# A four-layer transformer on one core: layer 1's attention placed beside the last expert outputs of layer 0

## The chip, the cores and the metric

The kernel runs on one core of a Trainium2 chip. The metric is the device time of one execution in microseconds (us); less is better. The engines are named as in the profile: PE (TensorE, matmul and transposition), DVE (VectorE), ACT (ScalarE), POOL (GpSimd, which here issues the indirect DMAs), SP (SyncE, which here only issues DMAs).

## What is computed

Input and output are 16 sequences of 256 tokens with 128 features, fp32. Four layers follow each other, each of the form x + mixer(norm(x)) + feedforward(norm(x)), with a norm that has no weights. The norm divides by a square root, and so does the one inside layer 0's mixer:

```python
def _layernorm(x, axis=-1, eps=1e-05):
    m = jnp.mean(x, axis=axis, keepdims=True)
    v = jnp.var(x, axis=axis, keepdims=True)
    return (x - m) / jnp.sqrt(v + eps)
```

- Layer 0: the mixer is a linear state-space recurrence over each sequence, feature by feature, followed by `W_out` and a bias `b_out`; it amounts to a causal convolution. The feed-forward part is a mixture of eight SwiGLU experts, two per token, with weights from a softmax over gate logits, and a ninth expert that is shared by all tokens.
- Layer 1: causal attention with 16 heads of 8, and a SwiGLU part with int8 weights that arrive as int32 and are scaled by 1/127.
- Layer 2: attention over a window of three tokens, and a feed-forward part with ternary weights.
- Layer 3: causal attention again, and a small coupling network, applied three times.

## The kernel before

The 4,096 tokens lie in SBUF for the whole time as eight blocks `X[i]` of 128 partitions x 4 x 128; a block holds two sequences. `HALVES` are blocks 0 to 3 and 4 to 7. A token group (one of the 4 columns of a block) has 128 tokens, so a half has 16 groups, called n. `xT[i]` is the transposed, normalised block, 128 features x 512 tokens, which feeds the projections and feed-forward matmuls.

The order of work:

1. `lag_weights` and `lag_sums` (L359 to L405) make the convolution's kernel: exponentials on ACT, products on DVE, matmuls `lag` on PE, eight copies `kt` (L395) on DVE, and a round trip through DRAM. `toeplitz` (L410) loads back a block of it in shifted form by SP's queue into a buffer with tag `toe`, of which there are five.
2. `prepare` (L192 to L239) makes for each half the statistics (`stats`, L113) and the inverse standard deviation (`inv_std`, L105: add, a square root on ACT, L109, a reciprocal on DVE), then a second norm factor `r1` and an offset `off` for the convolution's input Z, each in a chain of small DVE and ACT operations. ACT forms Z, PE transposes it (`zT`), and PE multiplies by the gate weights (`lg`). When all eight blocks have logits, `route` (L247) computes the slots of every token in a sorted buffer of 23 tiles of 256 slots per half, nearly all of it on DVE, with `tot` and `pos` on PE. Then ACT makes the normalised `xn` (L234), PE transposes it and ACT copies it to `xT`.
3. `scatter` (L341) writes the groups of `xn` into the sorted buffer `XS` by indirect DMA on POOL, one per group and choice.
4. A loop over eight blocks: `conv(q)` (L416), then `shared_expert(q)` (L438), while SP loads the next Toeplitz blocks.
5. The expert loop over 46 jobs (23 tiles x 2 halves). Step k issues a scatter of the second half (the first 17 steps), `fetch_weights(k + 4)` (L457, POOL, tag `we`, five buffers), from step 24 on `fetch_outputs(0, k - 24)` (L509: two indirect gathers from `YS` into buffers `yk`, on POOL), `fetch_slots` on SP, transpositions of the input, gate and up matmuls, in eight of the steps `mixed` (L524: the convolution's result times `W_out`, started by a matmul of the bias row with a row of ones), and `down_slots` (L492 to L505), which stores the outputs to `YS` on SP's queue. `combine` (L517) adds weighted outputs to X on DVE, two operations per group.
6. After the loop: 32 gathers and 16 combines for the second half.
7. The weight packs of layers 2 and 3 (L602 to L604, SP's queue), layer 1's integer weights `pk1i` (L829, POOL's queue) and their conversion (L833, three DVE operations); `norm_half` (L607) for both halves.
8. `attention` (L618) over 16 sequences s of layer 1 in a software pipeline: in step s it makes the maxima of sequence s (scores on PE, `M` reduced on DVE, L712, in three steps), the exponentials of s - 1 (scores again on PE, `E` on ACT, L754) and the context of s - 2. Then the SwiGLU part, and layers 2 and 3, which keep their form.

In the stages 4, 5 and 8 the order of PE, ACT, DVE is that of the program text (`manual_schedule`; in 4 and 5 SP too, in 5 POOL too); an engine takes its instructions strictly in that order. In the others a scheduler sets the order when the kernel is built. A DMA is issued by the engine whose queue it is on, in that engine's order.

Of the kernel before, what the change touches and what calls it, by code (L numbers as in the profile page):

```python
# [18 lines left out]
P = 128  # L19
B, S, D = 16, 256, 128  # L20
NBLK = 8
NT = 4
# [11 lines left out]
PK0 = dict(log_a=64, bpar=64, cpar=64, log_dt=64, dpar=32, lns=1, lnb=1, gate=8, gamma=128, beta=128, wout=128)  # L34
# [17 lines left out]
def program(ctx: ExitStack, tc: tile.TileContext, x, consts, consts0, rows, pk0, w0s, w0e, pk1, pk1i, pk2, pk3, out):  # L52
# [27 lines left out]
    def load(pool, src, spec, name, dt=F32, eng=None):  # L80
        cols, n = columns(spec)
        t = pool.tile([P, n], dt, tag=name, name=name)
        (eng or nc.gpsimd).dma_start(out=t, in_=src)
        return {k: t[:, s] for k, s in cols.items()}
# [9 lines left out]
    row = cp.tile([1, 3, D], F32, tag="row", name="row")  # L94
# [10 lines left out]
    def inv_std(pool, mv, n, name):  # L105

        r = pool.tile([P, n], F32, tag="rstd", name=name)
        nc.vector.tensor_scalar(r, mv[:, :, 1], EPS, None, ALU.add)
        nc.scalar.activation(r, r, AF.Sqrt)  # L109
        nc.vector.reciprocal(r, r)  # L110
        return r
# [42 lines left out]


    with banks(8, 0), tc.tile_pool(name="l0w", bufs=1) as wp, tc.tile_pool(name="l0", bufs=2) as sp:
# [10 lines left out]

        order = mybir.DependencyInfo(mybir.DependencyClass.NoSync, mybir.DependencyReason.DATA)
# [23 lines left out]
        def prepare():  # L192
# [6 lines left out]
            for hf, blocks in enumerate(HALVES):  # L199
# [4 lines left out]
                r1, off, off0 = (small(k, hf, HN) for k in ("r1", "off", "off0"))  # L204
# [3 lines left out]
                nc.scalar.activation(r1, r1, AF.Sqrt)  # L208
                nc.vector.reciprocal(r1, r1)
                nc.vector.tensor_tensor(r1, r1, r, ALU.mult)  # L210
                nc.vector.scalar_tensor_tensor(off, mv[:, :, 0], -1.0, r1, ALU.mult, ALU.mult)
                nc.vector.scalar_tensor_tensor(off0, mv[:, :, 0], -1.0, r, ALU.mult, ALU.mult)
                made.append((r, off0))
# [15 lines left out]
            routed = route(logits)  # L229
            for i in range(NBLK):  # L230
                r, off0 = made[i // 4]
                for t in range(NT):
                    k = i % 4 * NT + t
                    nc.scalar.activation(  # L234
                        xn[i][:, t, :], X[i][:, t, :], AF.Identity, bias=off0[:, k : k + 1], scale=r[:, k : k + 1]
                    )
                ps = transpose4(xn[i], f"xnT{i}")
                nc.scalar.copy(xT[i], ps)
            return xn, *routed  # L239
# [7 lines left out]
        def route(logits):  # L247
# [8 lines left out]
            m1, m2 = (wp.tile([P, N], F32, tag=k, name=k) for k in ("m1", "m2"))  # L256
# [58 lines left out]
            si = wp.tile([P, 2, N], I32, tag="slots", name="slots")  # L315
# [94 lines left out]
        def toeplitz(g):  # L410

            toes[g] = sp.tile([P, 4, 256], F32, tag="toe", name=f"toe{g}", bufs=5)
# [24 lines left out]

        def shared_expert(i):  # L438
# [18 lines left out]
        def fetch_weights(k):  # L457
            hf, j = jobs[k]
            w = live.setdefault(k, {})
            w["w"] = sp.tile([P, 6, 128], F32, tag="we", name=f"we{k}", bufs=5)  # L460
# [35 lines left out]
        def down_slots(k):  # L496
# [8 lines left out]
            nc.sync.dma_start(out=YS[hf][j * SLOTS : (j + 1) * SLOTS, :].rearrange("(t p) d -> p t d", p=P), in_=ys)  # L505
# [18 lines left out]
        def mixed(i):  # L524
            po = bank(f"po0_{i}")
            mm(po, ones, row[:, 0, :].unsqueeze(1).to_broadcast([1, NT, D]), True, False)
            for t in range(NT):
                mm(po[:, t * P : (t + 1) * P], yT[:, t % 2, 2 * i + t // 2, :], W0["wout"], False, t == NT - 1)
# [5 lines left out]
        xn, top, slots, rows_of, routed = prepare()  # L534
        for i in range(NBLK):
            affine(i)
# [11 lines left out]
        with tc.manual_schedule(engines=ordered):  # L548
            for g in range(4):
                toeplitz(g)  # L550
            for q in range(8):
                for g in range(4 * q + 4, min(4 * q + 8, 32)):
                    blocks_in = toeplitz(g)
                conv(q)
                add = nc.vector.tensor_tensor(X[q], X[q], xn[q], ALU.add)
                if q == 0:
                    tc.add_manual_dep(add.ins, routed.ins.name, order, reason="slots first")
                shared_expert(q)
            yT = wp.tile([P, 2, B, P], F32, tag="Z", name="yT")
# [5 lines left out]
        with tc.manual_schedule(engines=ordered | {mybir.EngineType.Pool}):  # L565
# [8 lines left out]
            up_slots(0)  # L574
            for k in range(NJ):
# [4 lines left out]
                out = k - TILES - 1  # L580
                if 0 <= out < HN:
# [580 lines left out]
```

## Time and profile before

| what | value |
|---|---|
| median of 3 runs | 1648.8 us (1647.44 to 1653.97) |
| the profiled execution | 1574.13 us, span 1572.4 us |
| mean granted TensorE clock in it | 0.935 |
| slots of all tokens ready (end of routing) | 76.9 us after the span's start |
| first expert matmul | 144.64 us |
| last expert matmul ends | 304.65 us |
| first reduction of a score maximum of layer 1 | 386.39 us |
| one sequence of layer 1's attention | 16.4 to 16.6 us |

All times inside the kernel are of one profiled execution, and count from the start of its span. A row of the timeline or of the chain reads: start, length, engine, line, operation, output <- inputs, and in brackets how long the engine had been idle and what released it. A row of the windows gives for each engine the busy us in that stretch and the number of its instructions, then the clock that TensorE was granted (1.00 is full speed), the share of time in which the DMA engines were busy, and GB/s.

### The profile page before, as it was taken

The numbers are of one execution on the slowest core, as the hardware profiler recorded it, in microseconds if no ns is written. First come the engines' busy times: TensorE is split into PE (matmuls) and PEld (weight loads), VectorE is DVE, ScalarE is ACT, GpSimd is POOL, SyncE is SP. The second block draws the span as 40 slices with busy tenths as digits, with TensorE's granted clock in tenths as the row PEclk, the third lists the DMA queues.
The fourth block names the chain that finished last, engine by engine and source line by source line (L and its number), as shares of the span: only waits on it lengthen the run. The fifth ranks groups of instructions, "written<-read, shape, count | busy, mean of one in ns | idle before, by whom it ended". The sixth has DMA issues, their size and how long they took to land.

```text
span 1572.4 us, 28051 instructions
## 1 busy us (share of the span) xinstructions
PE 1392.1 (89%) x11966; PEld 873.2 (56%) x11966; DVE 715.6 (46%) x1452; ACT 621.2 (40%) x951; POOL 268.5 (17%) x260
## 2 busy tenths in 40 slices
PE   3689999605999999999999999999899999998998
PEld 2557888503566666656555555455456666663434
DVE  6644334335555555334643234444355555532323
ACT  4712232104454545322433333443344545435453
POOL 1176437560000000000111011111000000001212
PEclk9999999856899999799999999999989999979888
DMA  8299677522000000000000000000000000000000
GB/s 283 65 327 308 184 205 214 143 77 86 2 2 2 2 2 2 2 0 1 1 0 1 1 0 1 0 0 1 1 1 2 2 2 2 2 2 0 7 21 28
DMA packets 67918, 77.85 MB, mean 50 GB/s; under 512 B 7633, under 2 KB 60114, under 8 KB 67154
## 3 DMA queue, kind: packets, MB, share of 16 engines
q1 hardware_dynamic: 59152, 47.37, 9.6%
q0 software_dynamic: 7920, 27.08, 6.0%
q8 instruction: 95, 1.56, 0.4%
q10 hardware_dynamic: 722, 1.60, 0.3%
q14 instruction: 29, 0.24, 0.1%
HBM read 55.39 MB, written 20.64 MB: 48 GB/s over the span
## 4 chain that ended last, share of the span: by engine, by line
PE 79%; DVE 7%; ACT 6%; issue 3%; DMA 3%; POOL 1%; SPq 0%; POOLq 0%; ACTq 0%; DVEq 0%
PE h L103 14%; PE se L103 8%; PE sc L103 8%; PE po L103 7%; PE c L103 6%; PE av L103 5%; ACT E L754 4%; DVE M L712 3%; PE mT L727 3%; PE sg L103 2%; PE su L103 2%; PE sy L103 2%; PE pq L103 2%; PE tw L103 2%; PE pv L103 2%
## 5 line engine op out<-in xcount | busy, mean ns | idle before, releaser
L712 DVE TENSOR_REDUCE M<-sc 128x4 f32<-128x1024 f32 (+3 forms) x256 | 195.9, 818 | 113.2 <-PE sc L103 113.2
L103 PE MATMUL h<-h,pk 128*128 128x512 f32 x512 | 221.0, 592 | 0.0
L754 ACT ACTIVATE E<-se 128x1024 f32<-128x1024 f32 (+1 forms) x192 | 158.8, 879 | 106.7 <-PE se L103 106.4
L103 PEld LDWEIGHTS h<-h,pk 128*128 128x128 f32 x512 | 97.3, 190 | 119.0 <-issue 115.3
L103 PE MATMUL sc<-Kp,Qm 32*128 32x192 f32 (+3 forms) x2048 | 135.7, 347 | 21.7 <-ACT E L754 21.5
L103 PE MATMUL se<-Q,Km 32*128 32x256 f32 (+3 forms) x2048 | 132.4, 345 | 12.1 <-DVE M L712 10.6
L103 PEld LDWEIGHTS sc<-Kp,Qm 32*128 32x128 f32 x2048 | 99.6, 197 | 70.7 <-ACT E L754 35.4
L881 POOL TENSOR_TENSOR pr<-q,k 128x512 f32<-128x512 f32 (+2 forms) x24 | 28.2, 1202 | 618.2 <-ACT k L874 440.7
L103 PEld LDWEIGHTS se<-Q,Km 32*128 32x128 f32 x2048 | 94.8, 194 | 51.3 <-issue 44.0
L1005 POOL TENSOR_TENSOR xT<-xT,c 128x512 f32<-128x512 f32 x24 | 30.2, 1280 | 442.3 <-DVE c L1004 442.2
L931 ACT ACTIVATE h<-h,pk 128x512 f32<-128x512 f32 x64 | 44.0, 687 | 144.1 <-PE h L103 144.0
L131 PE MATMUL xnT<-consts,xn 128*128 128x128 f32 x128 | 25.9, 349 | 69.6 <-DVE xn L122 69.6
L941 DVE TENSOR_TENSOR x<-x,po 128x512 f32<-128x512 f32 x8 | 5.5, 687 | 170.5 <-PE po L103 170.5
L103 PE MATMUL av<-E,vals 128*32 128x256 f32 (+3 forms) x2048 | 78.4, 306 | 0.0
L103 PE MATMUL c<-c,pk 128*64 128x512 f32 (+2 forms) x144 | 70.0, 635 | 0.0
L343 POOL DMA_INDIRECT XS<-xn,slots x64 | 63.9, 998 | 19.5 <-issue 17.1
L769 ACT COPY cu<-av 128x512 f32<-128x512 f32 x32 | 18.7, 585 | 121.2 <-PE av L103 121.2
L461 POOL DMA_INDIRECT we<-in_w0e,rows x46 | 46.2, 1004 | 117.1 <-DVE rows L330 64.8
L512 POOL DMA_INDIRECT yk<-YS,slots x64 | 60.6, 946 | 32.6 <-issue 14.9
L494 DVE TENSOR_TENSOR hs<-hs,su 128x512 f32<-128x512 f32 x46 | 31.6, 687 | 74.1 <-PE su L103 74.1
L996 ACT ACTIVATE c<-c,pk 128x512 f32<-128x512 f32 (+2 forms) x72 | 49.1, 682 | 40.2 <-PE c L103 40.2
L103 PEld LDWEIGHTS av<-E,vals 128*32 128x32 f32 x2048 | 53.1, 111 | 20.6 <-issue 2.9
(237 smaller groups left out, 2332.1 us busy)
## 6 DMA issues: line engine op xcount, KB each, us to landing
toe<-kd SPq DMA_DIRECT2D x32, 512.0 KB, 7.0
xs<-XS SPq DMA_DIRECT2D x46, 128.0 KB, 4.3
YS<-ys SPq DMA_DIRECT2D x46, 128.0 KB, 1.8
XS<-Z SPq DMA_DIRECT2D x4, 1024.0 KB, 12.3
pk<-in_pk SPq DMA_DIRECT2D x1, 3145.5 KB
x<-in_x SPq DMA_DIRECT2D x8, 256.0 KB
ycd<-yc SPq DMA_DIRECT2D x8, 256.0 KB, 5.6
yT<-ycd SPq DMA_DIRECT2D x4, 512.0 KB
```

The costliest lines, as they stand in the source:

```text
L103: nc.tensor.matmul(o, l, r, start=start, stop=stop)
L343: d = nc.gpsimd.indirect_dma_start(out=XS[hf][:, :], out_offset=at_rows(slots[:, k, hf * HN + n : hf * HN + n + 1]), in_=xn[HALVES[hf][n / ...
L461: nc.gpsimd.indirect_dma_start(out=w["w"].rearrange("p a b -> p (a b)"), out_offset=None, in_=w0e[:, :], in_offset=at_rows(rows_of[:, hf, ...
L494: nc.vector.tensor_tensor(h, h, pu, ALU.mult)
L512: nc.gpsimd.indirect_dma_start(out=y, out_offset=None, in_=YS[hf][:, :], in_offset=at_rows(slots[:, k, hf * HN + n : hf * HN + n + 1]),)
L712: nc.vector.tensor_reduce(dst, src, AX.X, ALU.max, negate=True)
L727: nc.tensor.transpose(ps[:, T, c * P : (c + 1) * P], negm[bl][:, c, T].rearrange("p g j k -> p (g j k)"), ident)
L754: nc.scalar.activation(E[:, 2 * n : 2 * n + 2, :], se[n][:, :, 0 : 2 * wide], AF.Exp, scale=ISQ)
L881: nc.gpsimd.tensor_tensor(pr[:, :, j:], q[:, :, j:], k[:, :, 0 : S - j], ALU.mult)
L931: nc.scalar.activation(hn[:, c, :], ps, AF.Gelu, scale=W2[sn][:, c : c + 1])
L996: nc.scalar.activation(h[i], ps[0:m], func, bias=bias[0:m], scale=scale)
L1005: nc.gpsimd.tensor_tensor(xT[i], xT[i], cpl, ALU.add)
```

## The change

- `inv_std` no longer takes a square root on ACT. `inv_sqrt` starts from a guess made of the number's bits and takes three Newton steps, eleven small DVE operations. `r1` is made in the same way.
- After the logits come eight Toeplitz loads and `conv(0)` and `conv(1)`, then `route`. `conv(q + 2)` follows `shared_expert(q)`. The buffers of the Toeplitz blocks and of the expert weights get one common tag with eight buffers.
- `xn` is made on DVE after the routing, not on ACT.
- `b_out` is added on DVE, block by block; its matmul in `mixed` goes.
- In the expert loop only groups 0 to 11 of the first half are fetched and combined. Blocks 0, 1 and 2 are normalised for layer 1 within the loop, one step of the generator `norm_steps` per job.
- The remaining 20 groups (12 to 15 of the first half and all of the second) are fetched and combined from a generator `rest`, which `attention` calls three times in each of its steps. It also normalises block 3, blocks 4 and 5, and blocks 6 and 7 as they become complete. `norm_half` is not called for layer 1 any more.
- `m1`, `m2` and `slots` move to the pool that lives to the end. The weight packs of layers 2 and 3 are ordered behind the last store of expert outputs.

```diff
     def inv_std(pool, mv, n, name):
 
+        v = pool.tile([P, n], F32, tag="rvar", name=f"v_{name}")
+        nc.vector.tensor_scalar(v, mv[:, :, 1], EPS, None, ALU.add)
+        return inv_sqrt(pool, v, n, name)
+
+    def inv_sqrt(pool, v, n, name):
+
         r = pool.tile([P, n], F32, tag="rstd", name=name)
-        nc.vector.tensor_scalar(r, mv[:, :, 1], EPS, None, ALU.add)
-        nc.scalar.activation(r, r, AF.Sqrt)
-        nc.vector.reciprocal(r, r)
+        a = pool.tile([P, n], F32, tag="rnew", name=f"n_{name}")
+        nc.vector.tensor_scalar(a.bitcast(I32), v.bitcast(I32), 1, None, ALU.logical_shift_right)
+        nc.vector.tensor_scalar(r.bitcast(I32), a.bitcast(I32), -1.0, float(0x5F3759DF), ALU.mult, ALU.add)
+        for _ in range(3):
+            nc.vector.tensor_tensor(a, r, r, ALU.mult)
+            nc.vector.scalar_tensor_tensor(a, a, -0.5, v, ALU.mult, ALU.mult)
+            nc.vector.scalar_tensor_tensor(r, a, 1.5, r, ALU.add, ALU.mult)
         return r
...
+    def norm_steps(pool, blocks, layer, into=None):
+        n = len(blocks) * NT
+        mv = pool.tile([P, n, 2], F32, tag="mvs", name=f"mv{layer}_{blocks[0]}")
+        for k, i in enumerate(blocks):
+            stats(pool, X[i], mv[:, k * NT : (k + 1) * NT, :], f"st{layer}_{i}")
+            yield
+        r = inv_std(pool, mv, n, f"r{layer}_{blocks[0]}")
+        for k, i in enumerate(blocks):
+            t = into(i) if into else pool.tile([P, NT, D], F32, tag="xn", name=f"xn{layer}_{i}")
+            normalise(t, X[i], mv, r, k * NT)
+            yield
+            ps = transpose4(t, f"xnT{layer}_{i}")
+            nc.scalar.copy(xT[i], ps)
+            yield
...
-            routed = route(logits)
             for i in range(NBLK):
-                r, off0 = made[i // 4]
-                for t in range(NT):
-                    k = i % 4 * NT + t
-                    nc.scalar.activation(
-                        xn[i][:, t, :], X[i][:, t, :], AF.Identity, bias=off0[:, k : k + 1], scale=r[:, k : k + 1]
-                    )
+                affine(i)
+            return xn, made, logits
+
+        def normalised(xn, made):
+            for i in range(NBLK):
+                mv, r = made[i // 4]
+                normalise(xn[i], X[i], mv, r, i % 4 * NT)
                 ps = transpose4(xn[i], f"xnT{i}")
                 nc.scalar.copy(xT[i], ps)
-            return xn, *routed
...
-            mm(po, ones, row[:, 0, :].unsqueeze(1).to_broadcast([1, NT, D]), True, False)
...
-        xn, top, slots, rows_of, routed = prepare()
-        for i in range(NBLK):
-            affine(i)
+        xn, made, logits = prepare()
+        for g in range(8):
+            toeplitz(g)
+        for q in range(2):
+            conv(q)
+        top, slots, rows_of, routed = route(logits)
+        normalised(xn, made)
...
+                nc.vector.tensor_tensor(X[q], X[q], W0["bout"].unsqueeze(1).to_broadcast([P, NT, D]), ALU.add)
                 shared_expert(q)
+                if q + 2 < 8:
+                    conv(q + 2)
...
-                out = k - TILES - 1
-                if 0 <= out < HN:
-                    fetch_outputs(0, out)
+                n = k - TILES - 1
+                if 0 <= n < 12:
+                    fetch_outputs(0, n)
...
-                down_slots(k)
-                if 0 <= out - 3 < HN:
-                    combine(0, out - 3)
-            for n in range(HN):
-                fetch_outputs(1, n)
-                if n >= 4:
-                    combine(1, n - 4)
-            for n in range(HN - 4, HN):
-                combine(1, n)
+                stored = down_slots(k)
+                n -= 4
+                if 0 <= n < 12:
+                    combine(0, n)
+                    if n == 7:
+                        norms.append(norm_steps(sp, (0, 1), 1, again))
+                    if n == 11:
+                        norms.append(norm_steps(sp, (2,), 1, again))
+                if norms and next(norms[0], True):
+                    norms.pop(0)
+            for f in norms:
+                for _ in f:
+                    pass
+
+        left = [(0, n) for n in range(12, HN)] + [(1, n) for n in range(HN)]
+        for hn in left[:6]:
+            fetch_outputs(*hn)
+
+        def rest():
+            waiting = left[6:]
+            for k in range(0, len(left), 2):
+                for hn in left[k : k + 2]:
+                    combine(*hn)
+                    if waiting:
+                        fetch_outputs(*waiting.pop(0))
+                yield
+                done = left[k + 1]
+                if done in ((0, HN - 1), (1, HN // 2 - 1), (1, HN - 1)):
+                    i = HALVES[done[0]][done[1] // NT]
+                    yield from norm_steps(fp, (i,) if done[0] == 0 else (i - 1, i), 1)
...
-    W2 = load(lp, pk2, PK2, "pk2", eng=nc.sync)
-    W3 = load(lp, pk3, PK3, "pk3", eng=nc.sync)
+    W2 = load(lp, pk2, PK2, "pk2", eng=nc.sync, behind=stored)
+    W3 = load(lp, pk3, PK3, "pk3", eng=nc.sync, behind=stored)
...
                         next(coming, None)
+                    if step < 2:
+                        next(beside, None)
                 if now:
                     shift(*now)
+                next(beside, None)
...
-            for blocks in HALVES:
-                norm_half(blocks, 1)
-            cTs = attention(sp, wp, range(NBLK), W1, 1)
+            cTs = attention(sp, wp, range(NBLK), W1, 1, rest())
```

## The prediction

> **What bounds the kernel now.** I read the page first: its 40 slices (about 39 us each) show where TensorE stops, and it stops for long in one place only.
>
> ```profile
> PE 1392.1 (89%) x11966; PEld 873.2 (56%) x11966; DVE 715.6 (46%) x1452; ACT 621.2 (40%) x951; POOL 268.5 (17%) x260
> ...
> PE   3689999605999999999999999999899999998998
> ...
> POOL 1176437560000000000111011111000000001212
> PEclk9999999856899999799999999999989999979888
> ```
>
> Elsewhere PE has nines: it bounds nearly the whole span. In slices 8 and 9 it has 0 and 5 while POOL has 5 and 6. The windows over that place (columns: PE, PEld, DVE, ACT, POOL busy; granted clock; DMA share; GB/s):
>
> ```profile
> 300.00:320.00 20.00, 4.66 (x33) 4.11 (x31) 5.48 (x13) 0.60 (x1) 9.40 (x10) 0.66 0.19 50
> 320.00:340.00 20.00, 0.00 (x0) 0.00 (x0) 5.61 (x16) 0.00 (x0) 15.12 (x17) 0.50 0.20 52
> 340.00:360.00 20.00, 0.00 (x0) 0.00 (x0) 6.65 (x36) 0.00 (x0) 6.24 (x7) 0.50 0.56 208
> 360.00:380.00 20.00, 9.85 (x35) 6.35 (x36) 14.46 (x75) 7.05 (x13) 0.00 (x0) 0.55 0.10 41
> ```
>
> The chain of waits through it (start, length, what):
>
> ```profile
> 302.65 2.02 PE sy L103 x16
> 305.14 1.77 DMA YS<-ys
> ...
> 346.54 2.57 DMA yk<-YS,slots
> 349.59 0.50 DVE st L117 x2
> 350.33 11.72 DMA pk1i<-in_pk1i
> 362.07 0.90 DVE pk1i L833 x3
> 365.89 4.12 DVE xn L122 x16
> 373.26 3.97 PE xnT L131 x15
> 377.23 1.50 PE pq L103 x2
> ```
>
> Half 1's last expert ends (T0, 304.65); its store lands; POOL then issues 32 gathers, one per 1.25 us, until 347.5; layer 1's integer weights, queued on POOL behind them, take 11.7 us; conversion and normalisation follow. The first score maximum starts at 386.39: 81.7 us after T0.
>
> Last, the front, where the change reorders most. DVE rows of the timeline:
>
> ```profile
> 19.12 0.16 DVE L211 SCALAR_TENSOR_TENSOR off<-mv,r 128x16 f32<-128x16 f32 x1
> ...
> 25.34 3.48 DVE L395 COPY kt<-lag 16x256 f32<-16x256 f32 x8 [4.92 <-PE lag L103]
> ```
>
> The first half's gate offsets (off) are ready at 19.12, long before DVE waits for the lag sums.
>
> **What the Trainium skill says.** "TensorE: Matmul & The Clock Gate", Part 1: The HAM clock gate: about 3.4 us without work puts TensorE at half rate, and about as long a busy stretch restores it. The trace agrees: 0.50 in the empty windows, 0.88 in 380 to 400. So the gap also costs a slow restart. "DMA: Bandwidth & Descriptors", the part on arbitration: an engine takes turns between queues packet by packet. The trace fits: pk1i was issued just after the two late weight packs on SP's queue and took 11.7 us at some 400 GB/s over all queues; a small load behind a big one shares, it doesn't wait its turn. "ScalarE: Activation LUTs", What ACT_TABLE_LOAD costs: 1.283 us a load and about as much of a drain; the trace has six loads of 1.283 us for L109, the drain it doesn't show apart.
>
> **The change, part by part.** I set it against the profiled execution, 1574.1 us with a span of 1572.4. The median shown, 1648.8, stands 75 us above; what makes that difference no view shows, so I carry the difference in us over unchanged.
>
> *Front, routing 11.5 us later.* In the changed order of DVE the eight kt copies stand ahead of the end of the first half's r1/off chain, so off waits for the lag sums: 25.3 + 3.5 for the copies + about 2 for ten small operations at 0.17 to 0.2 = 30.8, and the first Z activation at about 31. Before, Z stood ready from 21 and the first transposition ran at 25.08; blocks then follow every 3.7 us. The second half's chain stands after lg3's copy among 16 normalisations (0.262 each, 4.2) and some 33 operations in all, 5.5 to 6.5 us: its Z begins at about 53 against 41.5. The slots, ready at 76.9 before, come at about 88.4. If DVE's order hurt less, this is 5; if the normalisations collide with more, 15. ACT loses 32 xn activations and its Sqrt loads; none was on this path.
>
> *Scatters, shared experts, start of the experts: +10.* POOL's 47 scatters take 61.8 us (78.08 to 139.91, 1.315 each), so they end at 150.2. The first expert weights now stand behind all of them and land some 4.5 us later, 154.7. PE: eight periods of 8.55 less the two convs (2.24 each) done ahead, 63.9 from about 87.5, gives 151.4. The first expert matmul: 155 against 144.64. The two convs ahead of routing are thus worth nothing here: POOL is later. The eight bias additions on DVE (0.69 each) lie in periods of 8.55 in which DVE is half idle: nothing, 2 if not.
>
> *Expert loop: -10.* Eight bias matmul pairs go, 1.05 each (the row at 154.09 has 1.12 for a pair) = -8.4; 12 outputs instead of 16 gathered within it spare POOL 8 of the 1.25 us gathers, of which about 3.6 us was felt where PE waited for weights (6.3, 5.0 and 3.9 us at 245, 275 and 294). Norms of blocks 0 to 2 add 12 transpositions (0.17 each, 2 us of PE); their DVE share, 8 us, lies beside it. Sum -10 (-14 to -4): T0 at 305 to 306, +1.
>
> *The gap: -66.* After T0 no attention work waits for the second half's outputs; xT of blocks 0 to 2 is made. But three gathers on POOL need the last stores (T0 + 3.2, then 1.25 each) and stand ahead of pk1i, whose issue comes at about T0 + 8.2. The weight packs (3.8 MB) are issued from about the last store on and would take 9 to 10 us at 400 GB/s, so pk1i shares only their end: it lands at T0 + 14 (12 to 18). The three conversions (0.9) stand before the first maximum on DVE: T0 + 14.9 against T0 + 81.7, -66.8; I take -66. Projections and the first scores run under the wait.
>
> *Added within the attention: +12.* Combines left: 20 outputs x 2 x 0.36 = 14.6 us of DVE; stats of five blocks 1.75 each, 8.6; three Newton chains of 12 operations x 0.2, 7.2; normalisation 5 x 1.05 = 5.2: 35.6 us. PE 5 x 0.66 and ACT 5 x 0.59 besides. It is spread over 25 calls, three in each 16.5 us sequence, 8.3 sequences, 137 us. Before, DVE has idle of 1.6 ahead of step 1's maxima and 1.9 to 2.8 after them, but only 0.4 ahead of step 0's; a call adds 1.4 us. Two in three calls fit, the third is mostly felt: some 0.7 us of 1.4 eight times, 6, then 3.3 for the transpositions on the full PE, and about 3 for clock dips (0.79 to 0.91 already at 640 and 395). Taken 12; from 6 (all hidden but PE) to 25 (two thirds felt). POOL's 28 remaining gathers, 1.25 each, lie under sequences in which POOL is empty; what is combined was issued three calls earlier, at least 10 us, against a landing of 2.5.
>
> *Elsewhere: -2.* The Sqrt loads at layer ends are replaced by chains of the same length (2.2 before, 12 x 0.19 after); layer 1's feed-forward loses about 1.
>
> Sum: +1 - 66 + 12 - 2 = **-55**: span about 1518, median 1648.8 - 55, about **1594**.
>
> **Rivals.**
> *Less felt.* DVE is 55% busy in the attention, and slack of a buffer covers each call: the added work costs 5, the loop saves its full 14: -67, 1582. For it: the windows give DVE 20.6 to 23.3 of 40 us. Against: the row before step 0 has hardly any idle.
> *The start is late.* pk1i shares with the packs for all its time (lands T0 + 22), routing is 15 late, and 25 us are felt: -28, 1621. For it: the 11.7 us landing before. Against: the packs have a lead of 5 us.
> *Slower: the clock halves.* The gate measures PE's bubbles. If calls on DVE delay each maximum by a microsecond or two, so that PE has pauses in every sequence, PE may run at half rate for the 137 us that share. PE is busy 92% there, 127 us at 0.93; at 0.50 that is 236: +109, and in all +54, 1703. It decides once the mean clock of that stretch falls below 0.62 (127 x (0.93/c - 1) then exceeds 55 + 8). For it: the dips. Against: the longest bubble a call can make, 2 us, is under the 3.4 us.
> *It doesn't do what it says.* A combine in DVE's order could wait for a gather and hold the maxima: were each of the 14 outputs fetched late to wait 3.5 us, the gain would be gone. The three-call lead speaks against it.
>
> **How the numbers follow.** Forecast 0.52, less felt 0.24, late start 0.17, no gain 0.03, slower 0.04. The likeliest gives 1594. The range, 1566 to 1620, takes the first two with the bounds of their terms (-83 to -28) and the late start up to its own number; about 0.15 is left outside. A measurement here can't tell less than 0.5%, 8 us, from nothing: faster 0.94, same 0.02, slower 0.04.
>
> **What would show it.** Slots near 88, first expert near 155, T0 near 305, first maximum 15 us after T0; no PE gap over 20 us between 300 and 400; sequences of 17 to 18.5 us against 16.5 for the first eight, then as before; layers 2 and 3 as long as before. Wrong: routing not later, DVE rows with waits for yk within the attention, or a clock under 0.8 there.

## The result and the profile after

The changed kernel takes 1657.4 us (median of 20 executions, 1653.6 to 1668.9), the kernel before 1648.9 (20, 1646.1 to 1654.9): a ratio of 1.006, 95% interval 1.0042 to 1.0077. The forecast was 1594.

The chips on which these kernels ran are of two kinds. On chips 5 and 11 the kernel before took 1571.6 to 1576.2 us in every execution (on 11 at three different times), on chips 15 and 0 it took 1643.5 to 1654.1. The profile shown of before (1574.1) is of the first kind; the times beside it and the measured result are of the second. I call the first kind undisturbed. Whether this is a lasting property of a chip is not shown: all but chip 11 were used at one time only. What the second kind has in addition is shown below.

The page of the changed kernel, where it answers to the lines shown of before (40 slices of 41 us; busy tenths, and the granted clock):

```profile
PE   2644799767678889999999999999989999998999
...
POOL 1064244461130000000011111111000000000212
PEclk9976999798578899979999999999979999978898
```

The slices are counted from 0. The hole in slices 8 and 9 of before is gone, but there is one in slices 2 and 3 with 4 and 4 tenths, and PE stays at 6 to 8 tenths from slice 7 to slice 14. The chain of waits of the same profile, from the last expert's store to the first maximum of layer 1:

```profile
399.14 1.81 DMA YS<-ys
...
403.41 0.98 issue
404.39 0.94 POOL yk L542
...
405.63 0.95 POOL yk L542
...
406.59 7.58 DMA pk1i<-in_pk1i
...
415.09 1.15 DVE M L768
```

That is the transition much as forecast: gathers (four after the last store, where the forecast had three), then pk1i, then the maximum, 16.3 us after the last expert matmul, where before had 81.7. So the part that the change is about works, and what it gave, some 65 us, is more than given back elsewhere. This table, from the times of the named instructions, says where. The forecast stands in the last column; e0 and e1 are the two kernels profiled again, the first on a chip of the second kind, the second on an undisturbed one. In the second row pg is the first matmul of a shared expert and cv a matmul of a convolution; in the sixth, se are the second scores, those that the exponentials need.

| us | before, as shown | changed (e1) | before (e0) | changed, as measured | forecast |
|---|---|---|---|---|---|
| first scatter | 78.1 | 88.7 | 78.1 | 87.8 | 88 |
| first pg to last cv | 62.7 | 79.4 | 123.8 | 120.3 | see below |
| start to first expert matmul | 144.6 | 181.8 | 207.2 | 221.1 | 155 |
| expert loop | 160.0 | 146.4 | 172.6 | 177.6 | 150 |
| last expert to first maximum | 81.7 | 16.3 | 81.0 | 16.3 | 15 |
| first maximum to the 1,024th se of layer 1 | 243.0 | 268.9 | 237.6 | 291.9 | 255 |
| the rest | 943.0 | 943.3 | 947.5 | 949.7 | 941 |
| span | 1572.4 | 1556.8 | 1645.8 | 1656.6 | 1517 |

The second row lies within the third; rows three to seven add up to the span. The forecast's 63.9 us of matmuls ran up to the end of the last shared expert, so the second row has no number of it. The sixth row ends with the 1,024th of layer 1's 1,216 se matmuls, in the exponentials of the fourteenth sequence. The expectations below call it the last, but all that the change adds lies ahead of it. Up to the real last one the row reads 279.0, 305.2, 274.2 and 327.9, with the same differences to within 0.6 us.

One caution for what follows: in five other versions that leave the attention as it is (x3, x4, y1, z3, z4), all on undisturbed chips, the sixth row reads 273.6 to 274.7. TensorE spent 77 to 81 us of it at half clock there, and 63 in e1. So e1 is at the lucky end, and differences of 5 us from it in this row are not read.

### The profile page after: what moved, and what is told of

Same layout as the page of the kernel before. It is cut to its first block, busy times and chain, and to the rows that moved or that the text cites. A ratio compares the mean times of both kernels' runs of the same rounds, so it can differ in the third digit from the quotient of the medians.

```text
span 1656.6 us, 28124 instructions
## 1 busy us (share of the span) xinstructions
PE 1431.3 (86%) x11950; PEld 899.4 (54%) x11950; DVE 743.4 (45%) x1626; ACT 593.8 (36%) x900; POOL 266.3 (16%) x260
## 4 chain that ended last, share of the span: by engine, by line
PE 74%; DVE 9%; issue 5%; ACT 5%; DMA 3%; another core or an unknown queue 3%; POOL 1%; SPq 0%; POOLq 0%; DVEq 0%; ACTq 0%
PE h L107 13%; PE se L107 8%; PE sc L107 7%; PE po L107 6%; PE c L107 5%; PE av L107 5%; ACT E L810 3%; DVE M L768 3%; PE mT L783 3%; PE sy L107 2%; PE sg L107 2%; PE su L107 2%; PE pq L107 2%; DMA toe<-kd 2%
## 5 line engine op out<-in xcount | busy, mean ns | idle before, releaser
L107 PE MATMUL se<-Q,Km 32*128 32x256 f32 (+3 forms) x2048 | 140.0, 355 | 28.8 <-DVE M L768 23.2
L107 PE MATMUL sc<-Kp,Qm 32*128 32x192 f32 (+3 forms) x2048 | 139.9, 360 | 26.5 <-ACT E L810 20.8
L107 PEld LDWEIGHTS sc<-Kp,Qm 32*128 32x128 f32 x2048 | 103.1, 206 | 76.3 <-ACT E L810 33.5
L107 PEld LDWEIGHTS se<-Q,Km 32*128 32x128 f32 x2048 | 99.2, 200 | 70.0 <-issue 57.8
L988 ACT ACTIVATE h<-h,pk 128x512 f32<-128x512 f32 x64 | 44.0, 687 | 144.2 <-PE h L107 144.1
L524 DVE TENSOR_TENSOR hs<-hs,su 128x512 f32<-128x512 f32 x46 | 31.6, 687 | 82.4 <-PE su L107 39.0
L107 PE MATMUL sy<-we,hs 128*128 128x128 f32 x368 | 51.7, 286 | 14.9 <-DVE hs L524 14.9
```

The lines of the kernel that those rows point to most:

```text
L107: nc.tensor.matmul(o, l, r, start=start, stop=stop)
L524: nc.vector.tensor_tensor(h, h, pu, ALU.mult)
L988: nc.scalar.activation(hn[:, c, :], ps, AF.Gelu, scale=W2[sn][:, c : c + 1])
```

## The experiments

**The two kernels again.** No edit.

> The kernel before, unchanged, profiled again beside its own timed executions. Theory A (the profile shown of before, 1574 us, is an execution that lacked something which nearly all others have): this execution's span comes out near 1647, and its trace has about 75 us of slow stretches that the first trace does not have. Theory B (the profiled execution is typical and only the timing adds 75 us): the span is near 1572 again while the time is near 1649.

The span was 1645.8 us: theory A. Matmul by matmul, e0 runs 1 to 3 us behind the first profile up to the second convolution and 63 us behind a little later; the expert loop adds 12 more, and some 5 of this are made up in the attention. The timeline of e0 on PE, in that stretch:

```profile
102.30 0.37 PE L103 MATMUL cv<-toe,Z 128*32 128x128 f32 x1 [0.99 <-issue]
105.10 0.37 PE L103 MATMUL cv<-toe,Z 128*32 128x128 f32 x1 [2.43 <-issue]
107.20 0.37 PE L103 MATMUL cv<-toe,Z 128*32 128x128 f32 x1 [1.73 <-issue]
109.31 0.37 PE L103 MATMUL cv<-toe,Z 128*32 128x128 f32 x1 [1.74 <-issue]
112.80 0.37 PE L103 MATMUL cv<-toe,Z 128*32 128x128 f32 x1 [3.12 <-issue]
115.60 0.37 PE L103 MATMUL cv<-toe,Z 128*32 128x128 f32 x1 [2.43 <-issue]
```

Where no load held it, a convolution's 64 matmuls took 2.3 us in the first profile. Here the second convolution took 60.8 us: one matmul follows another after 2.8, 2.1, 2.1, 3.5 and 2.8 us, all multiples of 0.70, and "issue" says that the profile shows nothing that they wait for. The other seven convolutions of e0 took 2.2 to 2.4 us. The granted clock is 0.59 over 77 to 150, but that is not it: eight sy matmuls took 1.05 us at full clock and 2.07 at half (the measured run, at 305.73 and 320.75), twice as long and not twenty-six times.

> The changed kernel, unchanged, beside the kernel before on the same chip. If this chip runs the kernel before in about 1574 us, as the last one did: the changed kernel near 1571 (the run whose 46 of 47 scatters kept their place took 1571), that is no gain. If it runs it in about 1647: near 1657. In both cases the stage from the first pg matmul to the last cv takes some 15 us longer than before, and sequences 1, 3, 4 and 7 of the attention 20 to 26 us.

This chip was undisturbed (1573.9 us for the kernel before): the changed kernel took 1557.5 (0.9892, 0.9864 to 0.9921), faster by 1.1%, more than expected there. So on the same kind of chip as the profile the direction was as forecast, and less than a third of the gain came (16 of 55 us).

**Which part costs the attention its time.** In x1 the call of combine is left out of the generator (below); in x2 its gathers are, and the combines read buffers that are there already:

```diff
                 for hn in left[k : k + 2]:
-                    combine(*hn)
                     if waiting:
                         fetch_outputs(*waiting.pop(0))
```

> The changed kernel, but the generator leaves out the 40 combining operations on DVE (the last 20 groups' expert outputs are not added); the gathers on POOL stay. In the changed kernel the stretch from layer 1's first score maximum (415) to its last exponentials' scores (707) took 292 us, in the kernel before, profiled again, 238. Theory A (TensorE is slowed while POOL issues indirect gathers): the stretch stays above 275. Theory B (DVE's added operations delay the maxima, TensorE gets bubbles and half its clock): it falls to 245 to 265.

> The changed kernel, but the generator issues none of its 28 gathers: its combines read the first six groups' buffers again, so the same DVE work is done with wrong data. Theory A: the stretch of 292 us falls to 245 to 255 (238 and the 12 us forecast). Theory B: it stays above 275.

Both numbers in these expectations were of a chip of the second kind, but x1 to x4 ran on an undisturbed one, so they have to be read against e1 (268.9 us in the table's sixth row) and the five versions with 273.6 to 274.7. Without the combines it was 265.0, without the gathers 274.4; x2 again on e1's chip (z2) gave 272.8:

> The changed kernel without the generator's 28 gathers (its combines read the first six groups' buffers, wrong data). On a chip with 1574 us for the kernel before: as last time, 1566 to 1568 or a little less, so the gathers cost nothing there. On one with 1647, theory A: sequences 1 to 5 of the attention fall from 21 to 27 us to the 17 to 24 us of the undisturbed chip; without A they stay.

The gathers cost nothing there that these runs can tell, and 14.6 us of combines cost 4 to 10. Most of what is left should be the norms. By sequence (time from one sequence's mT, the transposition of its maxima, to the next, and mean clock; sequences are counted from 0, and the column headed 1 holds the maxima of sequence 1) e1 shows where:

```
sequence     1           2           3           4           5           6           7           8
before   17.3 0.80   17.1 0.94   18.7 0.87   16.7 1.00   18.0 0.91   16.7 1.00   16.6 1.00   16.7 1.00
e1       23.6 0.68   17.1 0.96   21.5 0.82   21.3 0.90   20.6 0.83   16.6 1.00   24.1 0.79   17.2 0.99
```

1, 3, 4 and 7 have statistics, Newton chains or normalisations on DVE. 2 has combines alone, 5 combines and one transposition, and 6 combines and one block's statistics. So 5 is slow without a norm on DVE, and 6 is not slow with one. The timeline of e1 in sequence 1, DVE:

```profile
366.49 0.16 DVE L112 TENSOR_SCALAR v_r<-mv 128x4 f32<-128x4 f32 x1
...
368.67 0.16 DVE L124 SCALAR_TENSOR_TENSOR r<-n_r,r 128x4 f32<-128x4 f32 x1
368.87 1.11 DVE L136 TENSOR_SCALAR xn<-x,mv,r 128x128 f32<-128x128 f32 x4
369.90 2.47 DVE L768 TENSOR_REDUCE M<-sc 128x4 f32<-128x768 f32 x4
```

and PE:

```profile
368.14 0.44 PE L107 MATMUL se<-Q,Km 32*128 32x64 f32 x4
371.32 1.37 PE L107 MATMUL se<-Q,Km 32*128 32x64 f32 x28 [2.75 <-DVE M L768]
```

One call of the generator, the Newton chain and a normalisation, holds DVE from 366.49 to 369.9, 3.4 us; the maxima of step 1, whose scores PE had finished at 367.1, stand behind it, and PE waits 2.75 us for the PSUM pair that they free. At 373.1 the clock goes to a half for 3.4 us. (It had been at a half from 342.4 to 366.3 too, since the wait at the transition.) Elsewhere in e1, pauses of 2.02 us at 407, 1.85 at 422, 1.74 at 449 and 3.89 at 486 were followed by 6.8, 3.4, 6.8 and 10.2 us at half clock.

The one at 449 stands behind a call of two combines, not of a norm. What decides is the gap that a call falls into, and the profile of before shows that there are two kinds. These are two lines on DVE of sequence 3, what PE does then, and the maxima of step 1 in sequence 4:

```profile
438.63 1.00 DVE L653 TENSOR_SCALAR Km<-Kp,consts 128x512 f32<-128x512 f32 x2 [1.10 <-ACT Kp L651]
439.55 2.48 DVE L712 TENSOR_REDUCE M<-sc 128x4 f32<-128x768 f32 x4
...
440.98 1.37 PE L103 MATMUL se<-Q,Km 32*128 32x64 f32 x28 [0.44 <-DVE M L712]
...
456.24 2.48 DVE L712 TENSOR_REDUCE M<-sc 128x4 f32<-128x768 f32 x4 [1.62 <-PE sc L103]
```

In sequence 4, as in 2, DVE is idle for 1.62 us ahead of the maxima. In 3, as in 1, the next block's Km fills that place, and PE already waits 0.44 us for the maxima. A call behind step 0 stands just ahead of them. The pauses of e1 fit that: calls of 1.60 (statistics), 1.30 (combines) and 3.45 us in sequences 3, 5 and 7 gave 2.02, 1.74 and 3.89 us, each 0.42 to 0.44 more; a call of 3.45 us in sequence 4 gave 1.85, 1.6 less.

Two kernels test the length of the calls. y2 cuts the same work into pieces of about 1.1 us at most and puts two behind each step, none behind the shift, so size and place both change; in its core:

```diff
-                    yield from norm_steps(fp, (i,) if done[0] == 0 else (i - 1, i), 1)
+                if hn[1] % NT == NT - 1:
+                    yield from fine_steps(fp, HALVES[hn[0]][hn[1] // NT], 1)
...
-                    if step < 2:
-                        next(beside, None)
+                    for _ in range(2):
+                        next(beside, None)
                 if now:
                     shift(*now)
-                next(beside, None)
```

> The changed kernel with the generator cut into 60 small pieces (one combine, two of four statistics, three operations of the Newton chain, one normalisation, one transposition), two pieces after each of the three steps of a sequence, none behind the shift; each block has its own chain. The same work and 24 more small DVE operations. Theory B (a call of 1.8 to 3.5 us stands ahead of a maximum, PE waits 2 to 4 us and the clock halves): the sequences 1, 3, 4, 5 and 7 fall from 20 to 26 us to 17 to 19, the whole by 15 to 25 us. If the sum of DVE's work is what costs, not its pieces, it stays or grows.

1544.1 us (0.9807, 0.9779 to 0.9835), 13.5 below e1; the stretch fell from 268.9 to 255.7, though DVE had more operations. It is how the work is cut and placed, then, and not its sum. Of the sequences named, only 4 fell below the expected 17 to 19 us (16.2); 1, 3, 5 and 7 still took 19.6 to 20.8 at clocks of 0.76 to 0.91. They are the ones with Km. The timeline of y2 in sequence 3 shows what holds them:

```profile
397.35 1.00 DVE L733 TENSOR_SCALAR Km<-Kp,consts 128x512 f32<-128x512 f32 x2 [1.10 <-ACT Kp L731]
398.26 0.16 DVE L198 TENSOR_SCALAR v<-mv 128x4 f32<-128x4 f32 x1
...
399.35 2.48 DVE L792 TENSOR_REDUCE M<-sc 128x4 f32<-128x768 f32 x4
...
400.77 1.37 PE L107 MATMUL se<-Q,Km 32*128 32x64 f32 x28 [1.52 <-DVE M L792]
```

The two pieces from 398.26 hold DVE for 1.09 us, PE waits 1.52, again 0.43 more, and at 403.6 the clock goes to a half for 3.4 us. The same happens in 1, 5 and 7 (1.74, 1.52 and 1.52 us). No run moves these pieces elsewhere, so this is read from the trace and not tried.

q2 leaves the norms out altogether and only transposes:

> The changed kernel; in the generator blocks 3 to 7 are transposed without being normalised (no statistics, no Newton chain, no normalisation: 21 us of DVE left out), with as many calls as before; gathers, combines and transpositions stay. Theory B (the calls of 1.8 to 3.5 us ahead of a maximum): first maximum to the last exponentials' scores falls from 269 to 246 to 252 us and no sequence has over 19 us, with a clock of 0.9 and more. If the combines or the transpositions are what costs: it stays above 260.

q2 (1635.9 us) fell on a chip of the second kind, so its partners are the measured run of the changed kernel, 291.9 us, and q1 below, on q2's chip and with the same attention, 290.9: it took 267.5, that is 23 to 24 less, where 17 to 23 were expected. Sequences 4 and 7, 21.3 and 23.1 us with the norms, took 16.7 and 16.6. But 2, 3 and 5 stayed at 26.1, 24.1 and 22.3, with no norm in them. 5 has the pause of 1.74 us behind two combines, as in e1. In 2 and 3 the pauses are put down to "issue" and "remote", while POOL issues gathers; e1's sequence 2 took 17.1 on an undisturbed chip. So that remainder is most likely of the kind of chip.

**The stage of the shared experts.** On the undisturbed chip this stage grew from 62.7 to 79.4 us, and the first expert came 27 us later than forecast. SP's queue in the timeline of e1 (start, time that the issuing took):

```profile
97.27 0.36 SPq L462 DMA_DIRECT2D ycd<-yc  x1
97.72 2.17 SPq L440 DMA_DIRECT2D toe<-kd  x4
110.33 0.36 SPq L462 DMA_DIRECT2D ycd<-yc  x1
110.78 2.60 SPq L440 DMA_DIRECT2D toe<-kd  x4
123.65 0.36 SPq L462 DMA_DIRECT2D ycd<-yc  x1
124.10 2.47 SPq L440 DMA_DIRECT2D toe<-kd  x4
```

and PE:

```profile
119.52 0.84 PE L107 MATMUL cv<-toe,Z 128*32 128x128 f32 x16 [0.29 <-DMA toe<-kd]
122.12 0.84 PE L107 MATMUL cv<-toe,Z 128*32 128x128 f32 x16 [1.75 <-DMA toe<-kd]
```

The four loads of a convolution's blocks go out at once, with hardly a wait for their buffers, but only after the store of the convolution before (ycd) is out, which waits for that convolution: SP waited 63.7 us in all for ACT's copy of the result (yc) between 85 and 170, and 3.2 ahead of the loads. So loads and convolutions take turns, some 13 us a round, and the DMA engines are partly idle in between: their share is 0.68 over 90 to 150, where the kernel before has 1.03 over 76 to 138. y1 puts the loads one convolution further ahead:

```diff
         for q in range(2):
             conv(q)
+        for g in range(8, 16):
+            blocks_in = toeplitz(g)
...
-                for g in range(4 * q + 8, min(4 * q + 12, 32)):
-                    blocks_in = toeplitz(g)
...
                 if q + 2 < 8:
                     conv(q + 2)
+                for g in range(4 * q + 16, min(4 * q + 20, 32)):
+                    blocks_in = toeplitz(g)
```

> The changed kernel with the Toeplitz loads issued one convolution earlier: 16 before the expert stage instead of 8, and those of conv(q + 4) behind conv(q + 2). Theory D (SP's queue: the store of conv(q + 2)'s result stands ahead of the loads of conv(q + 3), so the DMA engines are idle while PE convolves): the stage from the first pg to the last cv falls from 79 us (on the undisturbed chip) to 55 to 60, the first expert matmul comes 18 to 25 us earlier, and the whole 18 to 25 us. If POOL's scatters set the stage's end, as forecast, nothing changes.

1537.5 us (0.9765, 0.9692 to 0.9839), 20 below e1; its two executions, 1532.8 and 1542.2, lie 9 us apart. The stage took 51.3 us, and the first expert matmul came at 155.6: the 155 of the forecast, and for its reason, since PE was done 5.7 us earlier and waited for the expert weights behind POOL's scatters. Of these 26 us the profiled execution kept 16.5; its attention had 274.5 us for e1's 268.9. The windows of e1 over 90 to 150:

```profile
90.00:150.00 60.00, 47.79 (x439) 30.55 (x438) 21.73 (x26) 9.29 (x17) 45.86 (x47) 0.90 0.68 211
```

and of y1:

```profile
90.00:150.00 60.00, 55.68 (x572) 38.84 (x572) 32.43 (x37) 12.52 (x22) 46.59 (x45) 1.00 0.83 254
```

PE does 572 matmuls for 439 at a full clock, and the DMA engines carry 254 GB/s for 211.

**Both edits.**

> Both edits. Theories D and B: the two gains add up, 33 to 48 us below the changed kernel, which would beat the kernel before by 2 to 3% on either chip.

> The version with both edits, on another chip. If the chip runs the kernel before in 1574 us: 1530 again. If in about 1647: theory A (TensorE is slowed while POOL issues indirect DMAs) gives 1610 to 1635, since the same scatters and gathers stay; if the two edits take away what the change lost there, 1590 to 1610.

1530.1 and 1532.2 us (0.9718, 0.969 to 0.9746; 0.9749, 0.9707 to 0.9791), both on the undisturbed chip: 27 and 25 below e1, where 33 to 48 were expected. In the profiled executions the gains nearly add up: 16.5 (y1) and 13.8 (y2) make 30, and y3 had 27.7.

**The scatters, and TensorE's slow stretch.** In x3 the dependency holds one of the 47 scatters alone, so its 1573.1 us say nothing of the others; z4 holds all:

```diff
+                d = scatter(0, n, k)
+                tc.add_manual_dep(d.ins, added.ins.name, sync, reason="shared experts first")
...
+            d = scatter(1, *nk)
+            tc.add_manual_dep(d.ins, added.ins.name, sync, reason="shared experts first")
```

> The changed kernel, but the 47 scatters on POOL start only when the last shared expert is added to X. Theory A: without indirect DMAs beside it the stage of shared experts and convolutions (first pg matmul at 87 to last cv matmul at 207, 120 us in the changed kernel) takes 60 to 70 us; the first expert matmul then waits for the scatters, near 220. Theory C (TensorE is slow there for a reason of its own, power or the convolution's many small matmuls): the stage still takes over 110 us and the first expert comes near 275.

> The changed kernel with all 47 scatters behind the last shared expert's addition (in the earlier run of this kind only the first was held). On a chip with 1574: first pg to last cv falls a little from 79 us, since the loads have the DMA engines alone, to 65 to 75; the scatters then take 60 us alone, so the first expert comes near 240 and the whole is 50 to 60 us slower. On one with 1647, theory A: the same 65 to 79 us instead of 120; if TensorE is slow for a reason of its own: still over 110.

z4 ran on an undisturbed chip: stage 69.1 us and 1608.4 in all, as expected; the first expert came at 216.5, earlier than the 240 expected, because the first jobs need the first half's scatters alone. So 10 us of the stage's 79 go with the scatters beside it; that it is their DMA traffic beside the loads is likely and not shown. q1 does the same to the version with the loads ahead:

> The version with the loads ahead alone, and all 47 scatters behind the last shared expert. On a chip with about 1573 us for the kernel before: the stage from the first pg to the last cv stays at 51 us (TensorE sets it), and the scatters, now alone, make the whole 55 to 65 us slower. On a chip with about 1647: 51 to 60 us if the slow stretch belongs to POOL's scatters, over 90 if not.

q1 did fall on a chip of the second kind (1648.6 us for the kernel before, and as much for q1, whose first expert had to wait until 201.4). The windows of q1 over its stage:

```profile
89.00:140.00 51.00, 47.76 (x529) 33.04 (x528) 29.50 (x32) 11.59 (x20) 6.14 (x7) 1.00 0.74 224
```

and of y4, on the same chip, with the scatters beside it:

```profile
77.00:128.00 51.00, 27.08 (x184) 14.33 (x183) 12.25 (x20) 5.02 (x8) 37.95 (x38) 0.74 0.34 110
```

Without the scatters (seven indirect DMAs are left at its end) the stage took 51.2 us, the same as on an undisturbed chip, at full clock; with them 103.2. And the slowness went where the scatters went: q1's lie beside the first jobs, and jobs 1 to 23 took 79.9 us, where every other version of the change took 72.4 on either kind of chip, z4 with the same order too. The slow stretch on this kind of chip belongs to POOL's scatters. By what way they reach TensorE, no view shows: the DMA engines are two thirds idle in it.

**The same in the loop's tail.** From job 24 on POOL issues gathers and weights with hardly a pause. Jobs 24 to 45 (from the last sy of job 23 to that of job 45) took 72.9 us in the profile first shown, 69.2 in e1, but 85.4 in e0 and 100.4 in the changed kernel as measured. Its timeline on DVE there:

```profile
320.01 0.69 DVE L524 TENSOR_TENSOR hs<-hs,su 128x512 f32<-128x512 f32 x1 [12.35 <-remote]
```

"remote" is an event that no visible instruction gives at that time. Its two inputs were there 5 us earlier: the su matmuls ended at 314.3 and ACT's half of hs at 314.9. So it is not TensorE alone that is held. x4 (and z3, the same again) and r1 leave gathers out (x4 in the loop, r1 in the loop and in the generator); x4's core:

```diff
-                if 0 <= n < 12:
+                if n == 0:
                     fetch_outputs(0, n)
```

> The changed kernel, but in the expert loop only the first group's outputs are gathered and all twelve combines read them (wrong data, same DVE work), so POOL issues 2 gathers there, not 24. Jobs 24 to 45 took 100 us in the changed kernel, 86 in the kernel before profiled again, 73 in the profile first shown. Theory A: they fall to 63 to 68 us (2.84 a job and the norms). Theory B (the norms in the loop cost it): they stay over 85.

> The changed kernel with 2 of the loop's 24 gathers (wrong data). On a chip with 1574: jobs 24 to 45 take about 68 us, as before. On one with 1647, theory A: under 70 us instead of 100; without A: over 90.

> The version with all three edits, with 2 of the loop's 24 gathers and none of the generator's 28 (the combines read buffers of other groups: wrong data, the same DVE work). On a chip with about 1649 us for the kernel before: theory A gives jobs 24 to 45 in 63 to 70 us (100 in the version with the gathers) and no attention sequence over 21 us up to the eighth (21 to 23); without A both stay. On a chip with about 1573: jobs 24 to 45 near 66, the attention as with the gathers.

All three fell on undisturbed chips. Jobs 24 to 45 took 67.6 us in x4 and 67.5 in z3 against 69.2 in e1, and 65.9 in r1 against 70.4 in r2 beside it; r1's 1515.1 us are 1.6 below r2's: on such a chip POOL's gathers are nearly free. That they cost the 15 to 30 us on the other kind is likely by what q1 shows of the scatters, and was not shown.

**The front.** y4 takes y3 and puts both square roots of layer 0's preparation back on ACT; one of them:

```diff
-                r1 = inv_sqrt(sp, r1, HN, f"r1_{hf}n")
+                nc.scalar.activation(r1, r1, AF.Sqrt)
+                nc.vector.reciprocal(r1, r1)
```

> The version with both edits, and in layer 0's preparation the square roots on ACT as in the kernel before (both for the standard deviation and for the second norm factor); elsewhere the Newton steps stay. By the forecast of the front: DVE's chain is done before the kt copies again, so the first zT matmul comes near 25.5 instead of 32, the first scatter at 77 to 79 instead of 89, the first expert at 144 to 147 instead of 156; the whole 9 to 12 us below the version with both edits (about 1520). If something else delays the routing (the convolutions and loads ahead of it, normalisation on DVE), under 4 us.

> The version with all three edits beside it. On a chip with about 1649 us: 1625 as before. On a chip with about 1573: 9 to 12 us below the 1530 of the version with two edits, 1518 to 1522.

The first zT came at 25.1 us for 31.7, the first scatter at 77.9 for 88.6, the first expert at 144.1 for 155.1. r2 took 1516.7 us (0.9642, 0.9614 to 0.967), 13.4 below y3, a little more than expected: the Newton steps delayed the routing by 11 us, as forecast. y4 fell on a chip of the second kind and took 1625.0 against 1648.6 there (0.9864, 0.9834 to 0.9893). So this version beats the kernel before on both kinds of chip, by 3.6 and 1.4%.

## Why the prediction was wrong

Three steps failed. The measured kernel is 63 us slower than forecast. Of these, 39 are there on an undisturbed chip too (55 us forecast, 16 gained), from the first expert and the attention; 25 come with the kind of chip.

- *The transition, -66.* Right: 65.4 us on an undisturbed chip and 64.6 on the other kind (e0 against the measured run), with pk1i landing 15.5 us after T0 for the 14 forecast, and the first maximum at 16.3.
- *The routing 11.5 us later.* Right: 10.6 (78.1 to 88.7), and y4 shows the cause.
- *The first expert at 155.* Wrong, and the largest miss on an undisturbed chip: 181.8. The step took "eight periods of 8.55 less the two convs" for granted. The period came from a profile in which the loads ran ahead of the convolutions; that the store of conv(q + 2) now stands ahead of the next loads on SP's queue was not followed. With the loads ahead (y1) the number was right to within a microsecond.
- *The expert loop, -10.* Right in size on an undisturbed chip (-13.6). Jobs 1 to 23, with the bias matmuls, took 82.4 us before and 72.4 after; 8.4 were forecast for that. The other term was not what was said: 32 gathers lie ahead of T0 in both kernels, so POOL was spared none. The 3.7 us of jobs 24 to 45 have no cause shown.
- *Added within the attention, +12.* 26 in e1 and 31 in five other versions, beyond the bound given (25). The term that failed is "two in three calls fit". The "1.6 ahead of step 1's maxima" is there in every second sequence only; in the others Km fills it, and PE already waited 0.44 us. And a call was priced at 1.4 us, the combines' size, but the norms' calls hold DVE for 1.6 to 3.4 us; they were averaged into the same 35.6 us.
- *Against the halved clock: "the longest bubble a call can make, 2 us, is under the 3.4 us".* Wrong twice: the longest in e1 was 3.89 us, and 1.74 was enough for a half clock to follow. The Trainium skill, "TensorE: Matmul & The Clock Gate", Part 1: The HAM clock gate, speaks of an idle window of about 3.4 us; in these traces shorter pauses were followed by a half clock, and the measurement decides. The rival had the right mechanism at a fifth of its size: sequences 1 to 7 of e1 took 24 us more than in the first profile, the waits among them, at clocks of 0.68 to 1.00; the rival had 109.
- *The difference of 75 us, carried over "unchanged".* This made the sign wrong. It was no constant beside the kernel. e0 was slower than the first profile in two places where POOL issues indirect DMAs with hardly a pause: 61 us in the stage of the shared experts and 12 in the loop's tail. On such a chip the changed kernel loses 41 us in the stage (120.3 for e1's 79.4), 31 in the loop (177.6 for 146.4) and 17 to 23 in the attention (291.9 for 268.9 to 274.7), where the kernel before has no indirect DMA and loses nothing. For the stage the scatters are shown as the cause; for the loop and the attention the gathers are the likely one. What was gained on the undisturbed chip, 16 us, became a loss of 8.5.

The range missed the result by 37 us. On an undisturbed chip 1557.5 would itself have been a change of -16, outside -83 to -28. (The late start's own terms, 8 us for pk1i, 3.5 for the routing and 13 in the attention, add up to -30.5 and not to its -28.)

## What to carry to other kernels

When a profiled execution and the times beside it differ by several per cent, find out what the times have and the profile hasn't before anything is forecast from the profile: here it was a kind of chip, and the change added to what seems to be slow there. When a step is moved ahead, follow its store and its loads through the issuing queue: a store that waits for a result holds back every load behind it. And work that is to hide in an engine's gaps is priced by its longest piece against the gap where it stands, in each turn of the loop in which the gap differs, not by its sum against all gaps.

## What the runs showed of the hardware that was not expected

- On some chips TensorE's instructions come in steps of 0.70 us and multiples, for 60 us (e0), while POOL issues scatters back to back (one per 1.26 us). On such a chip the stage took 51.2 us without the scatters (q1) and 103.2 with them (y4). The granted clock in the records (0.5 to 1.0) doesn't show it.
- In the attention, pauses of 1.5 to 2.9 us on PE at full clock were followed within about 3 us by 3.4 us or more at half clock, with one exception in all runs (2.56 us at 368.1 in x1).
- 28 gathers beside the attention cost less than the scatter between versions on an undisturbed chip (272.8 and 274.4 us without them, 268.9 to 274.7 with them).
